# Image rows of a Fourier layer's first pass: loaded from GpSimd's queue instead of SyncE's

## Chip, cores and metric

The kernel runs on one core of a Trainium2 chip. Times are device microseconds (us) of one execution, median over runs. The engines are named as in the profile: PE (TensorE matmul), PEld (TensorE weight load), DVE (VectorE), ACT (ScalarE), POOL (GpSimd) and SP (SyncE). A "q" behind a name (SPq, POOLq) marks the engine's sequencer, which issues DMAs.

## The reference

For each of 64 images of 256 x 256 pixels the reference computes four Fourier layers on 32 channels, and then one transformer layer on the resulting 256 rows of 256 values plus 77 text rows. Cut to what matters here:

```python
h = jnp.concatenate([x, gx, gy], axis=-1)          # pixel, row grid, column grid
v = h @ p_w + p_b                                  # 3 -> 32 channels
for i in range(4):
    x1 = _fourier_layer(v, W1, W2)                 # rfft2, mix 24 x 12 modes, irfft2
    x2 = einsum('bcxy,cd->bdxy', v, w_w[i]) + w_b[i]
    v = x1 + x2
    v = (v - mean) * rsqrt(var + BN_EPS) * bn_g[i] + bn_b[i]   # over all images
    if i < 3: v = relu(v)
out = squeeze(einsum('bcxy,cu->bxyu', v, q_w) + q_b)
```

All is float32. The mean and variance run over all 64 images, so each layer is one pass over all images before the next can begin.

## The kernel before

**Stages.** `forward_first` loads all images once and computes the modes and moments that the first layer needs. Then for each layer `mix` multiplies the modes by the weights, and for the first three layers `layer(i, ...)` makes a pass over the 64 images. The last layer is folded into the transformer part, where `image_rows` reads the stored activations. This text is about `layer(0, ...)`, called the first pass; `layer(1)` and `layer(2)` are the second and third.

**One image of the first pass.** The image is cut into eight tiles of 128 partitions x 8 rows x 256 values (4 groups of rows x 32 channels on the partitions). The steps, with their lines:

- `am` (L599 to L613) loads the mixed modes of an image into `ams` on SP's queue (L601) and multiplies them by the scale on POOL (L609, twice per image).
- `lx` (L615 to L620, L627 to L629) loads the image's pixel rows into `mv`: four DMAs of 64 KB each, issued on SP at L617. Load n writes four partitions, 32n+24 to 32n+27, of 16 KB each. The other partitions of `mv` hold a table and the grid, loaded once (L576, 2 MB each). There are two `mv` buffers, for even and odd images.
- `sp`, `spT` (L641, L649) transform the modes along one axis on PE and transpose on DVE.
- `pre` (L661) makes a tile in PSUM: 16 matmuls per tile whose right side is `mv`, so that pixels, grids and modes are summed in one product. Tile t of image b reads `mv[b % 2]`.
- `evA`, `evB` (L684 on ACT, L686 on DVE, chosen per tile by the suffix a or d) apply relu and write the halves of the tile to `vo`. There are four `vo` buffers (pool "lo", L540), given to the tiles in turn in the order of `pre`.
- `st` (L693) stores a tile to DRAM with two DMAs of 512 KB on SP's queue.
- `prod`, `sqA`, `sqB` (L709 on PE, L720 on ACT) compute the next layer's product and its sum of squares; `turn` (L698, DVE), `y` (L731, PE), `zt` and `half` (L749, L741), `x`, `xo`, `xs` (L765, L776, L782) make the next layer's modes.

PSUM is a ring of four buffers of two banks, taken in the order of the steps.

**What sets the order.** The order is written out by hand in `ORDER[0]` (L128 to L135): one sentence of steps per image, where `@n` means "for the image n further on", or before if n is negative. The loop at L802 to L805 issues the steps in that order under a manual schedule, so every engine's queue, SP's and POOL's included, holds its share of the steps in the order of the sentence. Around the change it reads (two cut-outs):

```python
"spT1 pre2 sqB1 evA2.a st1 evB2.d st2 pre3 ... y2@-1 sqA2 turn0 am@2 sqB2 ..."
"... sqA3 pre4 half.a@-1 st6 zt0@-1 lx@1 evB4.a pre5 evA4.d prod4 evA5.a evB5.a turn4 sqA4 st3 sqB4 ..."
"... turn5 st5 pre7 evB7.a evA7.a prod5 sqB5 prod6 sqA6 st4 x@-1 sqB6 turn6 sqA5 pre1@1 st7 ..."
```

The tiles are made in the order 1, 0, 2, 3, 6, 4, 5, 7. With four `vo` buffers tile 7 takes the buffer of tile 3, so `evB7` and `evA7` may write only when the two stores of `st3` have landed. On SP's queue the steps of one image come in the order st1, st2, st0, am (for the image after the next), st6, lx (for the next image), st3, st5, st4, st7, with the small `xs` between, as far as the sentence goes; one image's sentence follows the other's. On POOL's queue there are, in the first pass, only the two multiplications of L609 per image.

At the start of the pass the modes and rows of images 0 and 1 are loaded ahead of the loop (L795 to L801): `load_am` twice, `load_x` twice, then `scale_am` twice.

Of the kernel before, what the change touches and what calls it, by code (L numbers as in the profile page):

```python
# [152 lines left out]
def tile_fno_fusion_transformer(ctx: ExitStack, tc: tile.TileContext, a, cst_d, grid_d, out):  # L153
    nc = tc.nc
# [370 lines left out]
    def layer(i, st, src, dst, acc):  # L525
# [7 lines left out]
        with ExitStack() as cx:  # L533
# [80 lines left out]

            def load_x(b):  # L615
                for n in range(4):
                    nc.sync.dma_start(  # L617
                        mv[b % 2][32 * n + 24:32 * n + 28],
                        x[b].rearrange("(j n s) y -> n j s y", j=4, n=4)[n],
                    )  # L620
# [6 lines left out]
            def lx(b, n, e):  # L627
                if b > 1:
                    load_x(b)  # L629
# [167 lines left out]
            if i == 0:  # L797
                for b in range(2):
                    load_x(b)
# [414 lines left out]
```

## Time and profile before

| what | value |
|---|---|
| median of 3 runs | 11783.08 us (11775.77 to 11795.58) |
| profiled execution | 11787.42 us |
| its span, first to last instruction | 11785.6 us |
| mean granted TensorE clock | 0.959 |
| busy share: PE, DVE, ACT, POOL | 91%, 72%, 55%, 11% |
| rows into `mv`: issues, size, queue | 256, 64 KB each, SP |
| first and last row issue (L617) | 189.1 us, 2867.6 us |
| stores of `vo` (all passes): issues, size, queue | 3072, 512 KB each, SP |
| SP's queue carries | 908160 packets, 3393.01 MB |
| POOL's queue carries | 40880 packets, 62.59 MB |

How to read the views used below. The page cuts the span into 40 slices of 295 us; each digit is a busy share in tenths. A line of the timeline is: start, length, engine, line, operation, output<-input, shape, count, and in brackets the idle time of the engine before it with what ended it. A line of the waits is: who <- for what: us in total, times, longest. A line of the window sums is: window and length, busy time and number of instructions of PE, PEld, DVE, ACT and POOL, then the granted TensorE clock, the mean share of the 16 DMA engines that were busy, and GB/s. The trace also holds every DMA packet with its start, length, size and kind of queue, but not the DMA engine that moved it.

### The profile page before, as it was taken

Reading aid. Unit: us, or ns where it says so; the run is one execution under the profiler, and the core shown is the slowest. Engines: PE = TensorE matmul, PEld = TensorE weight load, DVE = VectorE, ACT = ScalarE, POOL = GpSimd, SP = SyncE. Lnnn points to the kernel's source line nnn. Section 1 sums busy time; section 2 is a strip of 40 time slices with the busy share of each in tenths; the row PEclk is TensorE's granted clock in tenths of the full one; section 3 lists DMA queues with packets and bytes.
Section 4 is the critical chain, followed back from the end, with each engine's and each line's share of the span. In section 5 each row is a group of like instructions: output and inputs, shape, how many; then the busy total and the mean of one; then the engine's idle time right before and its main releaser. Section 6 shows DMA issues by size and latency. Waiting matters only on the chain. (4 is left out here: it accounts for less than half of the span.)

```text
span 11785.6 us, 408205 instructions
## 1 busy us (share of the span) xinstructions
PE 10764.6 (91%) x182038; PEld 5820.0 (49%) x182038; DVE 8458.3 (72%) x10405; ACT 6498.0 (55%) x10697; POOL 1326.6 (11%) x1987
## 2 busy tenths in 40 slices
PE   6888888888799999999969999999996899999998
PEld 3444444444344444444434444444443566666666
DVE  5777777777677777777767777777776666666665
ACT  5666666666556565656555666565564333333333
POOL 0000000000100000000010000000001233333333
PEclk7999999999899999999979999999998999999999
DMA  7555555555999999999989999999998655555553
GB/s 228 211 210 213 212 209 207 210 211 212 322 380 378 385 376 379 373 381 376 383 289 382 380 387 377 377 376 379 371 380 296 250 226 234 215 230 231 215 232 143
DMA packets 957949, 3485.44 MB, mean 296 GB/s; under 512 B 135960, under 2 KB 185496, under 8 KB 884888
## 3 DMA queue, kind: packets, MB, share of 16 engines
q1 hardware_dynamic: 908160, 3393.01, 75.3%
q0 software_dynamic: 40880, 62.59, 2.2%
q8 instruction: 1424, 23.33, 0.8%
q10 hardware_dynamic: 7144, 3.72, 0.1%
q14 instruction: 341, 2.79, 0.1%
HBM read 1761.87 MB, written 1696.92 MB: 293 GB/s over the span
## 5 line engine op out<-in xcount | busy, mean ns | idle before, releaser
L720 ACT ACTIVATE ring<-ring 128x1024 f32<-128x1024 f32 x3072 | 3116.2, 1015 | 1233.6 <-PE ring L709 1174.2
L698 DVE STREAM_TRANSPOSE t<-vo 128x2048 f32<-128x2048 f32 x1536 | 3464.8, 2286 | 20.8 <-DVE vo L686 0.5
L709 PE MATMUL ring<-vo,w 32*32 32x512 f32 x49152 | 2484.2, 618 | 303.9 <-ACT vo L684 287.1
L686 DVE TENSOR_SCALAR vo<-ring 128x1024 f32<-128x1024 f32 x1280 | 1545.0, 1221 | 1587.2 <-PE ring L672 790.0
L684 ACT ACTIVATE vo<-ring 128x1024 f32<-128x1024 f32 x1792 | 1792.0, 1022 | 1323.2 <-DMA v<-vo 565.3
L731 PE MATMUL ring<-t,cst 32*32 32x512 f32 x49152 | 2071.3, 599 | 48.8 <-issue 42.6
L709 PEld LDWEIGHTS ring<-vo,w 32*32 32x32 f32 x49152 | 805.9, 104 | 1315.0 <-ACT vo L684 589.5
L731 PEld LDWEIGHTS ring<-t,cst 32*32 32x32 f32 x49152 | 908.7, 103 | 927.9 <-issue 622.5
L609 POOL TENSOR_TENSOR ams<-ams,bns 48x512 f32<-48x512 f32 x384 | 401.0, 1044 | 8119.1 <-DMA ams<-mix 7538.2
L661 PE MATMUL ring<-cst,y 24*128 24x256 f32 x16384 | 1228.4, 402 | 77.1 <-DVE vo L686 61.1
L672 PE MATMUL ring<-vin,ws 32*32 32x512 f32 x32768 | 1279.6, 602 | 17.1 <-issue 12.2
L661 PEld LDWEIGHTS ring<-cst,y 24*128 24x128 f32 x16384 | 788.9, 185 | 989.0 <-DVE vo L686 391.7
L649 DVE STREAM_TRANSPOSE y<-ring 128x1024 f32<-128x1024 f32 x384 | 761.1, 1982 | 320.6 <-PE ring L641 319.6
L661 PE MATMUL ring<-mv,y 29*128 29x256 f32 x8192 | 726.9, 414 | 37.0 <-ACT ring L720 20.3
L765 PEld LDWEIGHTS ring<-cst,zt 128*128 128x128 f32 x4608 | 611.7, 216 | 227.1 <-ACT vo L684 113.9
L661 PEld LDWEIGHTS ring<-mv,y 29*128 29x128 f32 x8192 | 467.3, 191 | 378.2 <-ACT ring L720 210.1
L765 PE MATMUL ring<-cst,zt 128*128 128x96 f32 x4608 | 644.8, 304 | 7.0 <-DVE zt L749 7.0
L741 ACT COPY half<-ring 128x1024 f32<-128x1024 f32 x192 | 194.3, 1012 | 730.4 <-PE ring L731 730.4
L720 ACT ACTIVATION_READ_ACCUMULATOR ring<-ring 128x1 f32 x3072 | 585.3, 191 | 0.0
L1163 POOL DMA_DIRECT2D out_dram<-o x1024 | 504.2, 501 | 658.8 <-DVE o L1158 628.1
L749 DVE STREAM_TRANSPOSE zt<-ring 128x1024 f32<-128x1024 f32 x192 | 377.9, 1968 | 250.0 <-PE ring L731 250.0
L641 PE MATMUL ring<-ams,cst 49*128 49x512 f32 (+1 forms) x1536 | 450.8, 643 | 103.2 <-ACT vo L684 30.9
(366 smaller groups left out, 9654.2 us busy)
## 6 DMA issues: line engine op xcount, KB each, us to landing
v<-vo SPq DMA_DIRECT2D x3072, 512.0 KB
vin<-v SPq DMA_DIRECT2D x2048, 512.0 KB
ch<-v SPq DMA_DIRECT2D x512, 1024.0 KB
mix<-ob SPq DMA_DIRECT2D x96, 512.0 KB
ams<-mix SPq DMA_DIRECT2D x384, 96.0 KB
xin<-in_x_dram SPq DMA_DIRECT2D x16, 1024.0 KB
mv<-in_x_dram SPq DMA_DIRECT2D x256, 64.0 KB
out_dram<-o POOLq DMA_DIRECT2D x1024, 16.0 KB, 3.0
```

The source lines that it names most:

```text
L641: nc.tensor.matmul(ps[:, n, :], lhsT=EX[hv, 128 * h:128 * h + 128], rhs=ams[b % 2][hv], start=True, stop=True, skip_group_check=True,)
L649: nc.vector.transpose(y_[b, h].rearrange("p q c -> p c q"), ring[key][0][1].rearrange("p n (c k) -> p (n c) k", k=32),)
L661: nc.tensor.matmul(ps[n][:, 256 * r:256 * r + 256], lhsT=y_[b, t // 4][32 * n:32 * n + K, q:q + 4, :].rearrange("p q c -> p (q c)"), rhs=m ...
L672: nc.tensor.matmul(ps[n][32 * j:32 * j + 32], lhsT=ws[32 * n:32 * n + 32], rhs=v[32 * n:32 * n + 32, 2 * j:2 * j + 2, :], start=False, sto ...
L684: nc.scalar.activation(to, ring[key][h][1], AF.Relu)
L686: nc.vector.tensor_scalar(to, ring[key][h][1], 0.0, None, ALU.max)
L698: nc.vector.transpose(t32[b, t // 2][:, :, 8 * (t % 2):8 * (t % 2) + 8, :].rearrange("p y s c -> p s y c"), vo[b, t].rearrange("p s (y l) ...
L709: nc.tensor.matmul(ps[n][32 * j:32 * j + 32], lhsT=w4[i + 1][32 * n:32 * n + 32], rhs=vo[b, t][32 * n:32 * n + 32, 2 * j:2 * j + 2, :], st ...
L720: nc.scalar.activation(ps, ps, AF.Square, accum_out=acc[:, at:at + 1])
L731: nc.tensor.matmul(ps[n][32 * j:32 * j + 32], lhsT=FYT[32 * n:32 * n + 32, k, :], rhs=t32[b, j][32 * n:32 * n + 32, k].rearrange("p s c -> ...
L765: nc.tensor.matmul(ps[:, 0, 96 * g:96 * g + 96], lhsT=zt_[:, h, k0:k0 + 4, :].rearrange("p k c -> p (k c)"), rhs=FX[:, h, 48 * r:48 * r + ...
L1163: nc.gpsimd.dma_start(out[b, 64 * n + 16 * g:64 * n + 16 * g + 16].rearrange("(p t) d -> p t d", t=2), o[32 * g + 8 * n:32 * g + 8 * n + 8 ...
```

## The change

The four DMAs of `load_x` are issued by POOL (`nc.gpsimd`) instead of SP (`nc.sync`). Their place in the written order, their sizes, source and destination are the same. On POOL's queue they come after the two multiplications of `scale_am` that the sentence has before `lx`; at the start of the pass, the eight row loads of images 0 and 1 come ahead of the four multiplications.

```diff
@@ -614,7 +614,7 @@
 
             def load_x(b):
                 for n in range(4):
-                    nc.sync.dma_start(
+                    nc.gpsimd.dma_start(
                         mv[b % 2][32 * n + 24:32 * n + 28],
                         x[b].rearrange("(j n s) y -> n j s y", j=4, n=4)[n],
                     )
```

## Prediction

> **What bounds the kernel now.** I read the page's slices first, because they show the stages apart: the granted TensorE clock and the DMA engines' share.
>
> ```profile
> PEclk7999999999899999999979999999998999999999
> DMA  7555555555999999999989999999998655555553
> ```
>
> The row loads exist only in slices 1 to 10, the first pass (their issues run from 189 to 2868 us). There DMA is half busy and the clock is below full. The window sums of the first and second pass say it in numbers (busy PE, PEld, DVE, ACT, POOL; clock, DMA share, GB/s):
>
> ```profile
> 300.00:2900.00 2600.00, 2322.55 (x40662) 1216.86 (x40672) 1963.83 (x1094) 1693.97 (x2672) 125.40 (x122) 0.92 0.58 211
> 3100.00:5900.00 2800.00, 2678.27 (x57256) 1266.44 (x57248) 2102.45 (x1173) 1680.82 (x2649) 129.53 (x124) 1.00 0.98 379
> ```
>
> The first pass is not bound by DMA bandwidth, and PE (89%), DVE (76%) and ACT (65%) all have idle time. So I read who waits for whom from 300 to 2900 us, which is 61 images of 42.8 us:
>
> ```profile
> ACT vo L684 <- DMA v<-vo: 271.3, 66, 4.8
> ...
> PE ring L709 <- ACT vo L684: 233.2, 112, 4.1
> ```
>
> ACT's eviction waits for the landing of a store, about once per image and 4.4 us long, and PE's products wait for ACT. In the PE records each of the 61 images has exactly one gap over 0.7 us, 3.6 us on average. The timelines of SP, ACT and PE around one image show which store it is:
>
> ```profile
> 1536.18 0.82 SPq L693 DMA_DIRECT2D v<-vo  x2
> 1537.05 2.37 SPq L617 DMA_DIRECT2D mv<-in_x_dram  x4
> 1539.46 8.36 SPq L693 DMA_DIRECT2D v<-vo  x5
> ```
>
> ```profile
> 1551.97 1.94 ACT L684 ACTIVATE vo<-ring 128x1024 f32<-128x1024 f32 x2 [4.65 <-DMA v<-vo]
> ```
>
> ```profile
> 1547.42 1.71 PE L709 MATMUL ring<-vo,w 32*32 32x512 f32 x32
> 1553.05 2.92 PE L709 MATMUL ring<-vo,w 32*32 32x512 f32 x32 [3.93 <-ACT vo L684]
> ```
>
> I count from the first row issue, 1537.05 = +0. SP issues st6 (two stores) at -0.87, the four row loads, then st3 at +2.4 and +2.8. There are four vo buffers, so tile 7's eviction (evB7, evA7) writes the buffer that st3 reads. It is ready at +10.3 and starts at +14.9. Medians over the pass: +10.4 and +14.8.
>
> Why does st3 need 12 us? The packet records show it. Each row load is four packets of 16 KB. Four are in flight at a time, from +3.4 to about +11, one load after the other: the first takes 0.7 to 0.9 us per packet, the rest mostly 1.6 to 2.4. A 4 KB store packet takes 0.16. The DMA share says what the other engines do meanwhile:
>
> ```profile
> 1540.40:1543.00 2.60, 2.42 (x37) 1.68 (x30) 2.44 (x2) 2.25 (x4) 0.00 (x0) 1.00 1.02 329
> 1543.00:1545.00 2.00, 1.99 (x46) 0.75 (x40) 1.89 (x2) 1.66 (x2) 0.00 (x0) 1.00 0.27 47
> ...
> 1551.00:1554.50 3.50, 1.45 (x18) 0.42 (x32) 3.13 (x2) 2.52 (x3) 0.00 (x0) 0.86 0.29 117
> ```
>
> A share of 0.27 is 4 of 16 engines: twelve have finished st3 and idle while four still carry rows. Again 0.29 at the end: the same four work off stores that queued behind the rows. **The row loads hold four engines for 8 us, and st3 stands behind them in the same queue.**
>
> The gap also costs clock. Two images, each from row load to row load:
>
> ```profile
> 1152.60:1193.10 40.50, 35.97 (x659) 18.42 (x637) 31.22 (x19) 27.82 (x44) 1.81 (x2) 0.96 0.59 213
> 1491.40:1537.05 45.65, 41.24 (x672) 21.58 (x643) 31.77 (x19) 28.00 (x44) 2.09 (x2) 0.85 0.52 191
> ```
>
> In the clock records 26 images have 3.4 us at half clock and last 41.8 us on average; 10 have 13.7 us and last 45.5. So 1 us at half clock costs 0.35 us. The mean is 6.4 us per image. In the next two passes no PE gap exceeds 2 us, and the clock never halves.
>
> [...]
>
> **The change, part by part.**
>
> *SP loses four issues per image*, 2.37 us. Only st3 gains: it is issued at +0.0 and +0.4, since its data is long there.
>
> *POOL gains four issues per image.* In POOL's order they stand behind the two multiplications of L609, which wait for their own load:
>
> ```profile
> 1533.97 2.16 POOL L609 TENSOR_TENSOR ams<-ams,bns 48x512 f32<-48x512 f32 x2 [43.12 <-DMA ams<-mix]
> ```
>
> These end at -0.9 (median +0.0), and POOL then idles for 40 us. A POOL issue costs 0.5 us (row below), so 2 us behind nothing. From a POOL issue to its first packet took 1.2 us at 2924.6. So the rows reach the engines at about +1.2 to +2.7, not +3.4.
>
> *The rows change queue.* On the four engines st6 and st3 are 32 packets of 0.16 = 5.1 us, from about 0. If packets go by arrival, one row packet lies ahead of st3's end: 5.1 + 0.8 = 5.9. If whole transfers alternate, three do: 5.1 + 0.8 + 2.4 + 2.0 = 10.3. Both are at or before +10.4, where the eviction is ready. The stall goes. I take this as likeliest.
>
> *What that is worth.* 3.6 us of PE gap, and 6.4 x 0.35 = 2.25 us of clock: 5.85 us per image. What is late next: PE itself, busy 38.1 us per image, some 35.8 without the half clock. An image of 36.9 us would fill DVE (32.2) to 87%. For new small waits I take 0.9 us, a bit over the gaps of pass two (45 us over 0.7 us each in 2890 us, 0.7 per image), with bounds 0 and 2.0. So 62 images (the first two only fill the pipeline) x (5.85 - 0.9) = 307 us.
>
> *Rows' own due time.* The first matmuls that read them start at +22.9, in the shortened image at about +17. Rows land by about 8 + 5.1 = +13.4, or +18.5 if st5 and st4 also pass them. The second would cost up to 1.2 us, inside the bound of 2.0.
>
> *Start of the pass.* Eight POOL issues now precede the first L609 multiplications (189.5): 8 x 0.5 = 4 us later, once. Bounds 0 and 8.
>
> Sum: -307 + 4 = -303 us. The profiled execution took 11787.4 (span 11785.6), which gives 11484; against the median of 11783.1 it gives 11480. Bounds: 62 x 5.85 - 4 = 359 and 62 x 3.85 - 4 = 235, so 11424 to 11548.
>
> **Rivals.**
>
> *Packet-by-packet sharing.* If the engine alternates single packets, four row packets per engine (8 us) slip in among the first store packets, and st3 ends at 5.1 + 8 = +13.1, not +14.8. PE's gap shrinks by 1.7 us, worth 62 x 1.7 = 105 us, plus anything from none to all of the clock's 139. That is 11540 to 11680, middle 11610. For it: when stores arrived beside POOL's weight loads at 2884 us, about 13 store packets ran beside 16 load packets in 1 us. Against it: at 2879 to 2881 the stores already queued on four engines finished first.
>
> *The rows just get in front.* If they reach the engines ahead of st6, st3 ends at 1.2 + 8 + 5.1 = +14.3. That is what it is now: about 11765, no change.
>
> *Slower: rows in front, and longer.* Same place, but the four engines lose the overlap that hides the first load's packets: 16 packets at 2.4 on four engines are 9.6 us, so st3 ends at +15.9 and every image grows by 1.1 us, with 0.35 us per us of added half clock. That gives 11783 + 62 x 1.1 + 4 = 11855, and to 11900. It decides from 8.5 us of row time on (14.8 - 1.2 - 5.1), and only with rows ahead of st6. Against it: L609 ends 0 to 1.7 us after st6's issue, never before.
>
> [...] POOL's issues took 0.5 us (2.16 for four) while VectorE transposed SBUF to SBUF:
>
> ```profile
> 2876.81 2.16 POOL L386 DMA_DIRECT2D wn<-in_L_tok_fw_dram  x4 [52.51 <-PE ring L661]
> ```
>
> ```profile
> 2876.41 2.05 DVE L749 STREAM_TRANSPOSE zt<-half 128x1024 f32<-128x1024 f32 x1
> 2878.34 4.44 DVE L698 STREAM_TRANSPOSE t<-vo 128x2048 f32<-128x2048 f32 x2
> ```
>
> **How the numbers follow.** Stall gone 0.66; packet sharing 0.15; rows in front, no change, 0.09; slower 0.10[...]. A measurement of this kernel tells 0.2%, 24 us, from no change, so faster 0.81, same 0.09, slower 0.10. The range takes the first case and the second: 11415 to 11685.
>
> **What would show it.** Right: in the first pass the wait of L684 for v<-vo falls from 271 us to under 40, PE's gaps stay below 2 us, the clock of 300 to 2500 us is 0.98 or more, st3 follows st6 at once on SP, images last 37 to 38.5 us, and passes two and three keep their lengths. Wrong: the wait stays above 150 us (rows still ahead of st3), or a new wait of L661 for mv<-in_x_dram of over 1 us per image appears.

## The result, and the profile after

| | before | changed |
|---|---|---|
| median time, us | 11785.10 (4 runs, 11775.77 to 11795.58) | 11703.19 (4 runs, 11646.77 to 11727.0) |
| ratio to before, 95% interval | | 0.992, 0.9903 to 0.9937 |
| profiled execution, us | 11787.42 | 11646.77 |
| one image of the first pass, us (mean, from store to store of st6) | 42.8 | 40.8 |
| tile 7's wait for st3, us | 4.32 | 2.83 |
| half clock per image, us (300 to 2700 us) | 6.5 | 3.8 |

The changed kernel is faster by 82 us, where I had forecast 303. Its time is outside my range, 18 us above the upper end. Its four runs lie further apart than those of before, and the longer ones have the lower mean granted clock: 11646.77 us at 0.967, 11698.5 at 0.964, 11707.87 at 0.962, 11727.0 at 0.960. The profiled execution is the fastest of them, so a profile that shows 141 us stands for a median of 82.

The slices of the page, changed kernel:

```profile
PEclk7999999998999999999979999999997999999999
DMA  7656565657999999999989999999998655555553
```

The clock of the first pass is still mostly below full. The window sums of the first pass and of the second (busy PE, PEld, DVE, ACT, POOL; clock, DMA share, GB/s):

```profile
300.00:2800.00 2500.00, 2293.39 (x41303) 1199.56 (x41311) 1986.59 (x1105) 1713.12 (x2706) 247.71 (x369) 0.95 0.60 222
2950.00:5800.00 2850.00, 2730.55 (x58268) 1290.23 (x58270) 2139.73 (x1195) 1714.18 (x2700) 129.52 (x124) 1.00 0.98 379
```

0.95 instead of 0.92, and not the 0.98 or more that I had named as the sign of success. The second pass is as it was: the same clock, the same DMA share and the same 379 GB/s. The waits from 300 to 2850 us:

```profile
ACT vo L684 <- DMA v<-vo: 193.8, 81, 5.8
...
PE ring L709 <- ACT vo L684: 162.3, 111, 5.6
```

The wait for a store has shrunk from 271 to 194 us. It has not gone; I had said that over 150 us would show me wrong. The same image in the timelines of SP, POOL, ACT and PE, one after the other:

```profile
1520.04 3.17 SPq L693 DMA_DIRECT2D v<-vo  x4
```

```profile
1519.01 2.16 POOL L609 TENSOR_TENSOR ams<-ams,bns 48x512 f32<-48x512 f32 x2 [35.62 <-PE ring L661]
1521.11 2.04 POOL L617 DMA_DIRECT2D mv<-in_x_dram  x4
```

```profile
1534.44 1.94 ACT L684 ACTIVATE vo<-ring 128x1024 f32<-128x1024 f32 x2 [3.09 <-DMA v<-vo]
```

```profile
1531.44 1.71 PE L709 MATMUL ring<-vo,w 32*32 32x512 f32 x32
1535.52 2.06 PE L709 MATMUL ring<-vo,w 32*32 32x512 f32 x32 [2.37 <-ACT vo L684]
```

All that the edit does to the order of issue happened as planned: st6 and st3 go out back to back on SP, and POOL issues the four row loads in 2.04 us right behind its multiplications. But ACT still waits 3.09 us for st3's landing, and PE still has its gap, now 2.37 us. So st3 is issued sooner and still lands late. The row loads in the list of what touches `mv` (first line: shortest, median and longest issue in ns, first and last start):

```profile
L617 POOL DMA_DIRECT2D mv<-in_x_dram x256: 502/507/652, 182.0 to 2711.4; - x128
...
DMA to landing us min/median/max: 4.5/9.3/12.8
```

The window sums show where DMA stands while st3 is on its way and after it:

```profile
1525.50:1528.00 2.50, 2.31 (x38) 1.27 (x48) 2.39 (x3) 1.81 (x3) 0.00 (x0) 1.00 0.55 179
1528.00:1531.00 3.00, 3.00 (x50) 1.19 (x20) 2.98 (x2) 3.00 (x5) 0.00 (x0) 1.00 0.70 247
...
1534.00:1536.50 2.50, 0.98 (x13) 0.20 (x18) 2.50 (x2) 2.06 (x3) 0.00 (x0) 1.00 0.32 129
```

At the end, again only about 5 of 16 engines have work (0.32): some engines are behind the rest, as before. The trace has sixteen landing records for each store, which I take as one from each engine; those of st3's second store say which engines are late. In one image of each kernel (us):

```
before:  11 engines 1496.76 to 1496.90, one 1498.00;  the last four 1502.67  1503.98  1504.80  1504.96
changed: 12 engines 1447.46 to 1448.18;               the last four 1451.62  1452.64  1453.71  1454.10
```

**In both kernels twelve engines are done with st3 well before the other four (5 to 8 us before, 3 to 6 in the changed kernel), and those four carry the rows.** The last half of that is inferred, since a packet's record does not name its engine: though POOL issues all four loads within 2 us, no more than four row packets run at once (five for 1.1 of 405 us), and the later ones start as earlier ones end. The twelfth engine is a case of its own: in most images eleven are done together, at 7.0 to 7.4 before and 6.5 to 7.0 in the changed kernel on the axis below, and the twelfth follows at 8.4. One engine stays at 8.4 even where the rows come late (experiments 5 and 7: fifteen engines at 6.3 to 6.9, one at 8.3 to 8.4); why, no run shows.

From here on I follow three moments of st3's second store: issued, landed on its twelfth engine, landed on its last. They count from st6's first issue (0.87 us ahead of the prediction's +0), as medians over the pass. Before it is 3.6 / 8.4 / 15.6, in the changed kernel 1.7 / 8.4 / 14.2. On this axis tile 7 was ready to be evicted at 10.4 + 0.87 = 11.3; what lands by then costs nothing.

### The profile page after: what moved, and what is told of

It is laid out like the page before. It is cut to its first block, busy times and chain, and to the rows that moved or that the text cites. A ratio compares the mean times of both kernels' runs of the same rounds, so it can differ in the third digit from the quotient of the medians.

```text
span 11645.0 us, 408456 instructions
## 1 busy us (share of the span) xinstructions
PE 10694.7 (92%) x182038; PEld 5785.2 (50%) x182038; DVE 8456.8 (73%) x10405; ACT 6495.3 (56%) x10697; POOL 1461.2 (13%) x2243
## 5 line engine op out<-in xcount | busy, mean ns | idle before, releaser
L698 DVE STREAM_TRANSPOSE t<-vo 128x2048 f32<-128x2048 f32 x1536 | 3464.2, 2285 | 20.5 <-DVE vo L686 0.5
L609 POOL TENSOR_TENSOR ams<-ams,bns 48x512 f32<-48x512 f32 x384 | 401.0, 1044 | 7781.0 <-DMA ams<-mix 7293.6
L661 PE MATMUL ring<-cst,y 24*128 24x256 f32 x16384 | 1226.3, 402 | 74.9 <-DVE vo L686 59.5
L661 PEld LDWEIGHTS ring<-cst,y 24*128 24x128 f32 x16384 | 786.5, 184 | 988.5 <-DVE vo L686 389.4
L661 PE MATMUL ring<-mv,y 29*128 29x256 f32 x8192 | 717.2, 411 | 37.0 <-ACT ring L720 19.6
L765 PEld LDWEIGHTS ring<-cst,zt 128*128 128x128 f32 x4608 | 580.5, 207 | 206.8 <-ACT vo L684 113.9
L661 PEld LDWEIGHTS ring<-mv,y 29*128 29x128 f32 x8192 | 462.8, 189 | 372.9 <-ACT ring L720 210.8
L765 PE MATMUL ring<-cst,zt 128*128 128x96 f32 x4608 | 613.0, 294 | 7.3 <-DVE zt L749 7.3
```

Source lines behind the costliest of these rows:

```text
L661: nc.tensor.matmul(ps[n][:, 256 * r:256 * r + 256], lhsT=y_[b, t // 4][32 * n:32 * n + K, q:q + 4, :].rearrange("p q c -> p (q c)"), rhs=m ...
L698: nc.vector.transpose(t32[b, t // 2][:, :, 8 * (t % 2):8 * (t % 2) + 8, :].rearrange("p y s c -> p s y c"), vo[b, t].rearrange("p s (y l) ...
L765: nc.tensor.matmul(ps[:, 0, 96 * g:96 * g + 96], lhsT=zt_[:, h, k0:k0 + 4, :].rearrange("p k c -> p (k c)"), rhs=FX[:, h, 48 * r:48 * r + ...
```

## The experiments

**Theory A**: the stall is worth what I reckoned, but a second queue doesn't free the four engines: the rows still get through ahead of st3's last packets there. **Theory B**: what the change brought is SP's issue time alone (st3 issued sooner), and the rows' packets matter little. **Theory C**: the stall goes, and it is worth less than I reckoned, since something else comes next. Before's median beside the runs was 11780.08 us for the first four kernels, 11793.25 for the next four, 11793.07 for the last four. All the moments are collected in a table after the last experiment.

### 1. Rows on SP, but behind st3

The kernel before with the four loads moved behind `st3` in the written order.

```diff
-    "... half.a@-1 st6 zt0@-1 lx@1 evB4.a pre5 "
-    "evA4.d prod4 evA5.a evB5.a turn4 sqA4 st3 sqB4 ..."
+    "... half.a@-1 st6 zt0@-1 evB4.a pre5 "
+    "evA4.d prod4 evA5.a evB5.a turn4 sqA4 st3 lx@1 sqB4 ..."
```

> The kernel before with one word of the order moved: the row loads stay on SP's queue but come after the two stores of st3. Theory A (place on the four engines: what costs is that st3's packets finish after the rows' packets): st3 lands about 6 us after st6's issue, the wait of L684 for v<-vo falls below 1 us per image, the half clock goes, an image of the first pass takes 37 to 38.5 us and the kernel 11440 to 11560 us. Theory B (SP's issue time: the change gained because st3 is issued 2.4 us earlier on SP): the same as the changed kernel, 11650 to 11730, because st3 is issued as early and no earlier. Theory C (the stall was worth less than its length, because PE, DVE or ACT take over): the wait is gone but an image still takes 40 us or more, about 11650.

Measured: 11407.07 us, ratio 0.9678 (0.9662 to 0.9694); an image takes 36.7 us. The timeline of SP, then the window sum and the wait for stores from 300 to 2500 us:

```profile
1315.09 2.92 SPq L693 DMA_DIRECT2D v<-vo  x4
1318.06 2.78 SPq L617 DMA_DIRECT2D mv<-in_x_dram  x4
```

```profile
300.00:2500.00 2200.00, 2106.43 (x40314) 1105.40 (x40312) 1946.56 (x1081) 1669.34 (x2639) 123.28 (x118) 1.00 0.67 246
```

```profile
ACT vo L684 <- DMA v<-vo: 72.5, 83, 1.5
```

The same SP, the same four loads, the same four engines: only the order differs, and 373 us are gone. St3 has landed at 8.4, the clock is 1.00 and PE is busy 96% of the window. An image of 36.7 us isn't the 40 or more of theory C, which falls here. The wait that is left (72.5 us, at most 1.5 long) is another one: st4 lands at 20.5, as it did before, but the next image comes 6 us sooner now, and its tile 0 waits for st4, 0.9 us on ACT and 0.7 on DVE. Here the text ahead of the prediction has to be corrected: the buffers aren't handed on in the fixed turn of `pre`. Tile 7 takes tile 3's as stated, but the waits of the next image's tiles 1 and 0 name st5 and st4 in the kernel before, and st4 and st5 in the changed one.

### 2 and 3. A fifth buffer: before and changed

With five `vo` buffers in the first pass tile 7 no longer needs st3's. The sums of squares of all tiles go into four shared columns, to make room; so the scales of the later layers aren't the reference's.

```diff
-        ("lo", 4)
+        ("lo", 5 if i == 0 else 4)
```

> The kernel before with five vo buffers in the first pass instead of four, so that tile 7 no longer needs st3's buffer (room is made by letting the sums of squares of all tiles fall into four columns, so the later layers' scales are not the reference's). Theory A: the wait for v<-vo goes, with the rows still ahead of st3 on SP's queue: 11440 to 11560 us, image 37 to 38.5 us. Theory B: SP's queue is as it was, so little changes if issue time is the matter: 11750 or more. Theory C: wait gone, image 40 us or more, about 11650.

> The changed kernel with five vo buffers (same cut in the sums of squares). Theory A: the queue of the rows no longer matters once nobody waits for st3: the same time as the kernel before with five buffers, within 0.3%. Theory B: faster than that by what SP saves, up to 2.4 us per image, 150 us. Theory C: as with the kernel before with five buffers, at about 11650.

Measured: before with five buffers 11390.87 us, ratio 0.9666 (0.9651 to 0.968), 36.4 us per image; changed with five buffers 11403.24, 0.9674 (0.966 to 0.9689), 36.6 us. The window sum of before with five buffers:

```profile
300.00:2500.00 2200.00, 2138.00 (x40502) 1123.27 (x40500) 1953.83 (x1086) 1681.90 (x2657) 125.42 (x122) 1.00 0.68 248
```

PE is busy 97% at full clock, and evictions wait for a store only once in the window, for 2.7 us (in the other, 0.4 us per image are left on ACT). St3 lands as late as ever (15.7 and 14.5): the transfers are what they were, only nobody waits for them. So the stall is worth 6.4 us per image, and once it is gone the place of the rows' issue makes no difference to the time that is clear of the spread of the runs.

### 4. Sixteen loads of one partition each, on POOL

```diff
-                    nc.gpsimd.dma_start(
-                        mv[b % 2][32 * n + 24:32 * n + 28],
-                        x[b].rearrange(...)[n],
-                    )
+                    for j in range(4):
+                        nc.gpsimd.dma_start(
+                            mv[b % 2][32 * n + 24 + j:32 * n + 25 + j],
+                            x[b].rearrange(...)[n, j:j + 1],
+                        )
```

> The changed kernel with every row load cut by partition: sixteen DMAs of 16 KB per image on POOL's queue instead of four of 64 KB. If it is the number of DMA engines that makes the rows slow[...], the sixteen loads spread over all engines in small packets, the rows take 1 to 2 us of each engine, st3 lands 4 us earlier and the kernel takes 11450 to 11570 us. If it is the receiving side (64 KB in 2.4 us is 27 GB/s into four partitions, whoever sends), the rows still take 8 us, and now on more engines: no gain over the changed kernel, or a loss, 11690 to 11900. If the packets stay 16 KB on one engine each, the result lies near the changed kernel's. In each case POOL issues for 8 us per image, which nothing waits for.

Measured: 11403.48 us, ratio 0.9673 (0.9659 to 0.9687), 36.8 us per image. Its packets are of 1 KB, up to 16 of them run at once, and spread over 16 engines they are 1.0 us of each per image. St3 is issued at 1.7, as in the changed kernel, and lands at 9.4 instead of 14.2.

Theory B falls: st3's issue is the same in the changed kernel and here, yet the time differs by 300 us; and between before and changed, 1.9 us of earlier issue brought the eleven free engines 0.5 us forward and the twelfth none (8.4 and 8.4). Theory A stands so far. But this edit changes three things at once: the engines (16 for 4), the size of the packets (1 KB for 16), and the time over which POOL hands out the work (11 us instead of 2: 16 issues of 0.5 us, the later of them waiting for earlier loads to land: 188.4 us in 127 waits from 300 to 2600 us). The next runs separate them.

### 5. The rows on ACT's queue

The same four loads with `nc.scalar.dma_start`: another queue, without POOL.

> The row loads on ACT's queue instead of POOL's, at the same place in the order. If any second queue shares the four engines with the stores packet by packet (theory A), st3 lands as late as in the changed kernel and the time is 11600 to 11760 us. If something of POOL's queue itself[...] keeps st3 back, ACT's queue gives the whole stall back, 11400 to 11500. ACT issues the rows once its earlier work is done, at about st6 as well.

Measured: 11506.86 us, ratio 0.9753 (0.9739 to 0.9768), 38.2 us per image. ACT has evictions ahead of them in its order, so they are issued only at 4.6 to 5.8. St3 is mostly past by then and lands at 8.3. This was meant to tell whether POOL's queue itself keeps st3 back; with the rows issued so late it doesn't. Whether a burst on ACT's queue at POOL's moment would delay st3 as well is not shown. The waits from 300 to 2500 us:

```profile
ACT vo L684 <- DMA v<-vo: 133.4, 71, 3.2
DVE vo L686 <- DMA v<-vo: 129.2, 62, 3.2
```

The stall has moved: st4 lands at 20.2, and tile 1 of the next image waits for it, 2.05 us per image on ACT and 2.18 on DVE.

### 6. Three quarters of the rows

The changed kernel with `for n in range(3 if b > 1 else 4)`: the fourth load, a quarter of an image's rows, is left out.

> The changed kernel with three row loads per image instead of four (the fourth quarter of the rows of images from the third on is left out, so the output is not the reference's). Theory A: the four engines have 2 us less to carry, st3 lands at about +11.6 instead of +13.6, the wait falls from 2.9 to about 1 us per image, and the half clock mostly goes: 11400 to 11560 us. If st3 is held back by a fixed cost of the second queue and not by the rows' length, the wait stays near 2.5 us per image, 11650 to 11720.

Measured: 11451.01 us, ratio 0.9706 (0.9692 to 0.9721), 37.5 us per image; st3 lands at 12.3 instead of 14.2, and tile 7 waits 0.98 us. A quarter less to load brings st3's end 1.9 us nearer. So the rows' length does lie in the path of st3, though they are on another queue.

### 7. The burst, later

The changed kernel with eight fills of a spare tile on POOL ahead of the four loads, which then come at 5.5 to 7.0.

```diff
             def load_x(b):
+                for _ in range(8 if b > 1 else 0):
+                    nc.gpsimd.memset(pause, 0.0)
                 for n in range(4):
```

> The changed kernel with eight idle fills on POOL (about 4 us) ahead of each image's row loads, so that the rows reach the engines about 4 us later, when st3's packets are nearly done; nothing else moves. Theory A: later rows make the kernel faster, the wait for v<-vo goes and the time is 11390 to 11500 us. If what counts is how much the engines carry in an image and not the order, nothing changes: 11650 to 11730. If the rows had no time to spare, the kernel gets slower, with waits of L661 for mv<-in_x_dram.

Measured: 11538.32 us, ratio 0.9783 (0.9766 to 0.9799), 39.0 us per image. The waits from 300 to 2500 us (the edit shifts the lines by four: L688 and L690 are `evA` and `evB`):

```profile
ACT vo L688 <- DMA v<-vo: 156.3, 70, 3.7
...
DVE vo L690 <- DMA v<-vo: 150.8, 60, 3.8
```

As in experiment 5: st3 lands at 8.4, st4 at 20.7, and tile 1 waits 2.6 us. In experiments 1, 5 and 7 alike the burst spares st3, and st5's last engine is 5.1 to 5.4 us behind its twelfth. The rows here are on POOL's queue, in one burst, and st3 is spared all the same: it isn't POOL's queue as such that keeps st3 back. In each of these kernels the burst delayed one store or another; what differs is who needs that buffer first. In experiment 1 it is tile 0, which comes after tile 1.

### 8. Sixteen small loads, the same four engines

The changed kernel with each load cut into four by rows: 16 loads of 16 KB, each still four partitions, 4 KB packets.

```diff
+                    for q in range(0, 16, 4):
                         nc.gpsimd.dma_start(
-                            mv[b % 2][32 * n + 24:32 * n + 28],
-                            x[b].rearrange(...)[n],
+                            mv[b % 2][32 * n + 24:32 * n + 28, q:q + 4],
+                            x[b].rearrange(...)[n, :, q:q + 4],
                         )
```

> The control of the kernel whose rows are cut by partition: again sixteen loads of 16 KB on POOL's queue, but each goes to four partitions, so it stays on four engines in packets of 4 KB. If spreading over all engines was what helped there, this one keeps the stall: 11600 to 11760 us, with about four engines busy on rows for 8 us or more. If it was the smaller pieces or the slower pace of sixteen issues (8 us), this one is as fast: 11390 to 11480.

Measured: 11387.39 us, ratio 0.9652 (0.9638 to 0.9667), 36.4 us per image. St3 lands at 8.7. The four engines carry all of the rows as in the changed kernel, and the stall is gone all the same. The number of engines alone isn't what decides. Packet size or pace is left.

### 9. The same four large loads, paced

The changed kernel, its loads and 16 KB packets as they are, with four fills of a spare tile on POOL between one load and the next.

```diff
                 for n in range(4):
+                    for _ in range(4 if b > 1 and n else 0):
+                        nc.gpsimd.memset(pause, 0.0)
                     nc.gpsimd.dma_start(
```

> The changed kernel with four idle fills on POOL (about 2 us) between one row load of an image and the next, so that the same 16 KB packets come spread over 8 us, as the sixteen loads did. If it was the pace that let st3 through (fewer row packets waiting beside it), st3 lands at about +10 of st6's issue and its wait goes; the later rows then push st5 and st4 back and tile 1 waits for st4: 11400 to 11540 us. If it was the size of the packets, st3 still lands at +12 or later and the time is 11580 to 11720.

The timeline of POOL, the window sum of 300 to 2500 us, and the landing of the rows:

```profile
1529.54 0.56 POOL L621 DMA_DIRECT2D mv<-in_x_dram  x1
1530.13 2.27 POOL L620 MEMSET pause<- 128x512 f32 x4
1532.36 0.51 POOL L621 DMA_DIRECT2D mv<-in_x_dram  x1
1532.85 2.29 POOL L620 MEMSET pause<- 128x512 f32 x4
1535.09 0.51 POOL L621 DMA_DIRECT2D mv<-in_x_dram  x1
```

```profile
300.00:2500.00 2200.00, 2139.35 (x40580) 1124.33 (x40576) 1962.10 (x1090) 1685.18 (x2667) 619.20 (x1087) 1.00 0.67 248
```

```profile
L621 POOL DMA_DIRECT2D mv<-in_x_dram x256: 505/510/654, 184.0 to 2457.6; - x128
...
DMA to landing us min/median/max: 4.1/6.1/11.9
```

Measured: 11382.6 us, ratio 0.9656 (0.9641 to 0.967), 36.4 us per image; st3 lands at 9.0. The loads go out 2.7 us apart instead of 0.5, and that alone makes the changed kernel 321 us shorter. A load now takes 6.1 us from issue to landing, not 9.3. **In the changed kernel it is the burst that holds up the stores: with the queue, the engines and the packets' size as they are, spacing the loads frees st3 (last engine at 9.0 instead of 14.2).** The packet records show what the spacing does: in the changed kernel all 16 row packets of an image begin before st3's last engine is done, here 10 of the 16 (mean over the pass).

### 10 and 11. Eight loads, two sorts of packet

The changed kernel with each load cut in two: odd and even rows (pieces of 1 KB), or first and second half (packets of 8 KB). POOL hands them out over 4.7 and 4.0 us.

```diff
+                    for q in range(2):
                         nc.gpsimd.dma_start(
-                            mv[b % 2][32 * n + 24:32 * n + 28],
-                            x[b].rearrange(...)[n],
+                            mv[b % 2][32 * n + 24:32 * n + 28, q::2],
+                            x[b].rearrange(...)[n, :, q::2],
                         )
```

In experiment 11 `8 * q:8 * q + 8` stands in place of `q::2`.

> The changed kernel with each row load cut in two, even and odd rows: eight loads of 32 KB on the same four engines, in packets of 1 KB, issued within 4 us. If the engine alternates between the two queues packet by packet, a row packet of 1 KB costs a store packet little time and st3 lands at +8 to +9.5: 11380 to 11440 us. If packet size is of no matter, it equals the kernel with the loads cut in halves.

> The pair of the even and odd kernel: eight loads of 32 KB again, same issues and same pace, but in packets of 8 KB. Packet size: between the changed kernel and the even and odd one, st3 lands at +11 to +13: 11450 to 11620 us. Pace: the same as the even and odd one.

Measured: odd and even 11456.98 us, ratio 0.9716 (0.9699 to 0.9734), 37.5 us per image; halves 11487.85, 0.9744 (0.9729 to 0.9758), 37.8 us. The records show the odd and even pieces as packets of 4 KB, not of 1 KB as I had meant them to be. Nor are they on four engines: up to sixteen of them run at once (of the halves four, five for 1.4 of 415 us), and st3's landings show it, seven engines at 8.0 to 8.4 and the other nine at 9.5 to 11.6 (medians), where the halves have eleven by 7.0. So this pair differs in engines (16 and 4) as well as in size (4 KB and 8 KB), and st3 still lands at 11.7 and 11.9. The two times lie 31 us apart, but of the 32 us between the two profiled executions only 14 are in the first pass; the other 18 are in stages that the edit doesn't touch.

### 12. Eight loads on SP

Experiment 10 with `nc.sync`.

> The kernel before with its row loads cut into even and odd rows and kept on SP's queue, ahead of st3. [...]SP issues four more DMAs first: the stall stays, 11760 to 11860 us. If small packets as such make the rows fast (less than 5 us of the four engines), st3 lands earlier and the kernel is below 11650.

Measured: 11873.51 us, ratio 1.0071 (1.0056 to 1.0086), 44.3 us per image, the only kernel slower than before. The window sum of 300 to 2900 us:

```profile
300.00:2900.00 2600.00, 2283.39 (x39214) 1201.75 (x39212) 1894.36 (x1054) 1635.33 (x2573) 121.34 (x116) 0.89 0.57 203
```

In front of st3 in the same queue, smaller loads didn't help: st3 is issued at 7.7 instead of 3.6, its first twelve engines are done at 10.6, the last at 16.4, and the clock falls to 0.89. An issue 4.1 us later made the last engine only 0.8 us later. The rows themselves also take more of the four engines here, 9.0 us of each per image instead of 7.3 (in packets of 1 KB), so whether the 0.8 comes from SP's issues or from the rows the run doesn't tell.

### The moments together

| kernel | rows handed out over | st3 issued | 12th engine | last engine | image, us | time, us |
|---|---|---|---|---|---|---|
| before | 2.4 us, ahead of st3 | 3.6 | 8.4 | 15.6 | 42.8 | 11785.10 |
| 12: eight loads on SP | ahead of st3 | 7.7 | 10.6 | 16.4 | 44.4 | 11873.51 |
| changed | 2 us | 1.7 | 8.4 | 14.2 | 40.8 | 11703.19 |
| 6: three loads | 1.5 us | 1.7 | 8.4 | 12.3 | 37.5 | 11451.01 |
| 11: halves | 4.0 us | 1.7 | 8.4 | 11.9 | 37.8 | 11487.85 |
| 10: odd and even | 4.7 us | 1.7 | 10.1 | 11.7 | 37.5 | 11456.98 |
| 4: by partition | 11.0 us | 1.7 | 8.3 | 9.4 | 36.8 | 11403.48 |
| 9: paced | 8.8 us | 1.7 | 8.2 | 9.0 | 36.4 | 11382.6 |
| 8: by rows | 10.7 us | 1.7 | 7.7 | 8.7 | 36.4 | 11387.39 |
| 1: rows behind st3 | after st3 | 1.7 | 6.9 | 8.4 | 36.7 | 11407.07 |
| 5: on ACT | from 4.6 on | 1.7 | 6.7 | 8.3 | 38.2 | 11506.86 |
| 7: burst later | from 5.5 on | 1.7 | 6.5 | 8.4 | 39.0 | 11538.32 |
| 2: before, 5 buffers | as before | 3.7 | 8.4 | 15.7 | 36.4 | 11390.87 |
| 3: changed, 5 buffers | as changed | 1.7 | 8.4 | 14.5 | 36.6 | 11403.24 |

Read down the kernels from "changed" to 8, which all have the rows on POOL right behind its multiplications. With the same bytes, 2 us of handing out give 14.2, 4.0 to 4.7 give 11.7 to 11.9, and 8.8 to 11 give 8.7 to 9.4. Within the second and within the third group, packet size and number of engines (4 and 16 in each) move it by 0.7 us at most.

## Why the prediction was wrong

**The step that failed** is "*The rows change queue*". I took it that on the four engines at most three of the four row packets would lie ahead of st3's end, put that end between +5.9 and +10.3, and concluded: "The stall goes." On that axis it ended at 14.2 - 0.87 = +13.3, against +14.7 before. All sixteen row packets of the image began before that end, four on each of the four engines as far as the trace tells. My first rival, packet-by-packet sharing, said +13.1, and PE's gap shorter by 1.7 us; the gap fell by 1.1 (3.6 to 2.5 per image) and tile 7's wait by 1.5. I gave it 0.15. Its time, 11540 to 11680, was missed too, and that its landing came so near is in part luck: it counted 8 us of row packets on each engine, and they were 5.4. I had weighed two orderings that suited the change and a third that didn't, and had no row of the profile that told them apart.

The trace of the changed kernel agrees with that rival in that the rows' packets got in ahead of st3's last ones (all sixteen began before its last engine was done); single turns between the queues it doesn't show, so the ordering itself is not shown. The four late engines end st3 5.2 to 7.1 us behind the eleven free ones (medians), and the row packets account for 5.4 of it.

**What a row packet costs.** I used 0.7 to 2.4 us per 16 KB packet as if it were a property of the packet. Its mean was 1.82 us before, 1.35 in the changed kernel and 1.05 when paced. The sum over the four packets that an engine carries per image is 7.3, 5.4 and 4.2 us. When paced, each packet was shorter, and six of the sixteen came only after st3's end; how much each of the two does, the runs don't separate. The burst alone doesn't set the length either: in experiment 7, the same burst on POOL's queue but later, the mean is 1.76. Why a packet is longer or shorter no run shows. That the receiving side sets the length, one of the cases weighed for experiment 4, was my guess and is not shown.

**The worth of the stall** was right in mechanism and too small in size. I had 3.6 us of gap and 2.25 of clock, 5.85 us per image, less 0.9 for new waits, over 62 images 307 us. Experiments 1 to 3 took the stall away, by the order and by a fifth buffer, and gave 6.1, 6.4 and 6.2 us per image, 373 to 389 us in all. The allowance for new waits is the mis-sized term: in 2, 3, 8 and 9 at most 0.4 us per image of waits for stores on one engine came in the stall's place, and the image was shorter by more than 5.85 us all the same. With the stall gone the time lies below my range, so that error and the first have opposite signs. The times expected of experiments 1, 2, 4, 8 and 9 were too long in the same way, by 3 to 49 us; those of 7, 10 and 12 were too short by 38, 17 and 14 us.

**The gain that did come** adds up: 1.1 us of PE's gap and (6.5 - 3.8) x 0.35 = 0.95 us of clock make 2.05 us, and the image is shorter by 2.0. Over 62 images, less the 5.6 us of the later start, that is 121 us. In the profiled executions the second pass starts 132 us sooner; the other 9 of the 141 are in later stages. Without the clock's part the reckoning gives 63; the four runs lie between 58 and 138 below before's median, in the order of their clocks. From 300 to 2700 us every one of the 56 gaps of before (2.8 to 4.1 us) is followed by half clock; of the 58 in the changed kernel 40 are, 1.7 to 4.4 us long and 2.6 at the median, and 18 aren't, 1.6 at the median and none over 2.55. So the shortened gap lies where the clock goes either way, which would explain why its runs scatter.

The clock records show how gaps of the same length differ. Every change in them (172 records before, 136 in the changed kernel) lies a whole number of steps of 3.41333 us after the first, to within 0.02 us. Of the 114 gaps of the two kernels from 300 to 2700 us, each of the 96 with half clock behind it has 1.62 us or more of its idle time within one step of that grid, none of the 18 others has more than 1.53. In the changed kernel the gap of 2.50 us at 1368.9 us has at most 1.30 within one step and no half clock behind it; the one of 1.76 us at 1572.1 lies inside a step and has. In the other kernels the border lies between 1.5 and 1.9 us, but for two half clocks with less idle time before them. Nor does it hold in the later stages of the kernel before: gaps of 1.63 and 1.68 us inside a step had no half clock behind them in the second pass (at 5210.3 and 5691.3 us). And in the third, where I had said that the clock never halves, it did so three times for 3.4 us (from 7977.4, 8277.8 and 8755.6 us), with 1.37, 1.74 and 0.79 us as the longest PE gaps just ahead. What sets it no run shows.

**The rest held.** SP lost four issues, and st3 follows st6 at once, at +0.0 and +0.8 (I had +0.4 for its second store). POOL's issue took 0.507 us, 0.652 at most, behind nothing but L609. PE has no wait for `mv`, so the rows' due time was as harmless as reckoned. The first matmul of L661 starts at 201.4 instead of 195.8, 5.6 us later where I had 4. From POOL's issue to the first row packet I had 1.2 us, from a moment when the engines were idle; here it was 1.3 to 4.5 (median 3.0), with packets of st6 and st3 on the way at the same time; in experiment 7, later, 1.3 again. One reading of before was off: in the image shown the first row packet starts at +2.5, not at the +3.4 that I gave for all of them (median +3.3).

**Versions that beat both.** Experiments 8 and 9 keep the reference's computation and reach 0.9652 and 0.9656 of before; experiment 1, which moves one word of the order and adds no instruction, reaches 0.9678. Five buffers remove the stall almost completely and are no faster, so there is no more in it.

## What to carry to other kernels

Another issuing queue gave the rows no engines of their own here (st3's last engine at 14.2 instead of 15.6, its twelfth at 8.4 both times): look at when the transfer that someone waits for lands on each engine, and which other transfer sits on the last ones. Try such a load behind the store that is waited for, or handed out over the time in which it is needed: in the burst all 16 of an image's row packets began ahead of the store's end, and st3 landed at 14.2; behind st3 it landed at 8.4, and paced at 9.0. And if a gap on PE is only shortened, ask whether it still costs clock, as 40 of the 58 here did.

## What the runs showed of the hardware that I had not expected

- A 16 KB packet of the same load took 1.82 us on average on SP's queue, and on POOL's 1.35 in a burst beside st3, 1.76 in the same burst 4.5 us later and 1.05 when paced.
- One microsecond of SP's issue time was not one of landing: with st3 issued at 1.7 instead of 3.6, the engines without rows were done half a microsecond sooner, and the slowest of them at 8.4 both times.
- Four loads of 64 KB that went out within 2 us delayed the store queued beside them by about 6 us, and the same four 2.7 us apart by less than 1 (last engine at 14.2 and 9.0, against 8.4 where the burst comes after the store).
- Eight loads of odd and even rows ran on up to sixteen engines at once, the same bytes as first and second halves on four.
- In the records of the kernel before and the changed one the granted clock changed only at whole steps of 3.41333 us (308 records, to within 0.02 us). From 300 to 2700 us it halved after each of the 96 gaps with 1.62 us or more of idle PE within one step, and after none of the 18 with 1.53 or less; in later stages of the kernel before also after 1.37 and 0.79, and not after 1.63 and 1.68.
